# Gathers by index on GpSimd beside the second and third products of a graph network's second layer

## The chip, the cores and the metric

The kernel runs on one core of one Trainium2 chip. The metric is the device time of one execution in microseconds (us). The core has five engines that work side by side, each on its own list of instructions: TensorE (PE; PEld is its loading of weights), VectorE (DVE), ScalarE (ACT), GpSimd (POOL) and SyncE (SP). They wait for each other by semaphores. Transfers between the chip's memory (HBM) and the on-chip memory (SBUF) are done by 16 DMA engines; a transfer is issued from the queue of SP, ACT or POOL. Products are summed in PSUM.

## The reference

Four graph layers follow each other on x (4096 nodes x 128 features, f32) with one adjacency matrix adj (4096 x 4096, f32, mostly zeros); after each, x is replaced by the layer normalisation of x plus the layer's output.

```python
x = _layernorm(x + _L0_gnn_ref(x, adj, adj, L0_gnn_W, L0_gnn_a), axis=-1)
x = _layernorm(x + _L1_gnn_ref(x, adj, L1_gnn_W0, L1_gnn_b0, L1_gnn_W1, L1_gnn_b1), axis=-1)
x = _layernorm(x + _L2_gnn_ref(x, adj, ...), axis=-1)
x = _layernorm(x + _L3_gnn_ref(x, adj, ...), axis=-1)
```

The change is in the second layer, `_L1_gnn_ref`: two Chebyshev convolutions, each with an ELU behind it.

```python
def cheb_conv(x, L, W, b):
    Tx0 = x
    out = Tx0 @ W[0]
    Tx1 = L @ x
    out = out + Tx1 @ W[1]
    for k in range(2, W.shape[0]):      # W.shape[0] is 3
        Tx2 = 2.0 * (L @ Tx1) - Tx0
        out = out + Tx2 @ W[k]
        Tx0, Tx1 = (Tx1, Tx2)
    return out + b
h = jax.nn.elu(cheb_conv(x, L, W0, b0))     # 128 -> 256 features
h = jax.nn.elu(cheb_conv(h, L, W1, b1))     # 256 -> 128
```

Here L is adj. The first convolution multiplies adj by x and then by the result. The second is rearranged by the kernel: the weights are applied before adj, so it too takes two products of adj with a 4096 x 128 matrix. The layer therefore has four such products. The third layer is graph attention over 4 heads, the fourth a mean over neighbours.

## The kernel before

**Tiles.** x lies in SBUF as 128 partitions x 32 tiles of 128 features, beside its transpose xT. adj doesn't fit into SBUF, and each product reads it again, in chunks of 1 MB (`chunk`, L125 to L131): 512 rows by 512 columns, as 4 tiles of 128 rows. A chunk is loaded from SP's queue into one of five buffers of the pool `ld`; the load waits until the matmuls that read the buffer's last contents are done.

**The four products.** `propagate` (L656 to L668) runs one product: for each of 8 blocks of 512 columns it takes 8 chunks, and for each chunk 4 matmuls of 128x512, all summed in one PSUM tile, and then hands the block to the loop that called it. The first product (loop at L678) multiplies by x, and each block is transposed and copied to t1 by DVE (L681). The second (L684) multiplies by t1; in each block PE also applies the weights W1A (L690), ACT and DVE do the ELU (`elu`, L648), PE applies w2x (L695), and DVE copies the result to v (L697). The third (L707) multiplies by v; each block is transposed and copied to w by DVE (L711). The fourth is in the next part (L1126), where its blocks stand between the first steps of the third layer.

**The order of the work.** In this part a scheduler places the instructions, by the order of the program and their dependencies; instructions in `tc.keep_in_program_order` keep the order in which they are written. From the fourth product on, the order of PE, DVE, ACT and POOL is written out by hand (L1044). POOL's instructions of that part are the addition of a bias row to a block of x (L775, first of all), then products of attention weights with adj (L891, L892, L897, L898), and additions to x (L940).

**Memory that is used again.** The pools `l1w` and `l1h` hold the second layer's tiles. They are closed before the pool `l2w` of the third layer is opened, which uses the same memory: a tile of `l2w` (D, tau and others) waits for the last users of what lay there. The tiles t1, w and acc3 share one place (tag "yn"), as do v and hc (tag "v").

**What the change touches.** The lines before the loop at L678 (`wd`, `w2x`), and the ends of the three loops (after L681, L697 and L715). The first layer ends with the normalisation of x, block by block (`normalize`, L145 to L152; `normalize_x`, L154), whose last blocks are still done while the first product runs.

Of the kernel before, what the change touches and what calls it, by code (L numbers as in the profile page):

```python
# [11 lines left out]
F32 = mybir.dt.float32  # L12
BF16 = mybir.dt.bfloat16
I32 = mybir.dt.int32
AF = mybir.ActivationFunctionType
ALU = mybir.AluOpType
# [3 lines left out]
P = 128  # L20
IB = 512
TB = IB // P
# [11 lines left out]
def adj_resnorm_d4(ctx: ExitStack, tc: tile.TileContext, x_in, xT_in, adj, adjT, w0g, w0gT, a0, w1a, b1a,  # L34
# [7 lines left out]
    nc = tc.nc  # L42
    N, F = x_in.shape
# [17 lines left out]
    x = state.tile([P, NT, F], F32, name="x")  # L61
# [63 lines left out]
    def chunk(pool, src, ib, c, name="chunk", pinned=False):  # L125

        t = pool.tile([P, TB, IB], F32, name=name)
        r = nc.sync.dma_start(t, src[ib, c])
        if pinned:
            tc.keep_in_program_order(r)  # L130
        return t  # L131

    def transpose4(pool, name, src, order=lambda r: r):

        p = pool.tile([P, TB, P], F32, name=name)
        for k in range(TB):
            order(nc.tensor.transpose(p[:, k, :], src(k), ident))  # L137
        return p
# [486 lines left out]
    def network(usual):  # L625

        with ExitStack() as whole:
# [3 lines left out]
            with ExitStack() as first, ExitStack() as l1h_pool:  # L631
                ps_acc, ps_tr, ps_mm = [first.enter_context(tc.tile_pool(name=n, bufs=2, space=PSUM, reuse_waits="tile"))
                                        for n in ("ps_acc", "ps_tr", "ps_mm")]
                if not usual:
                    layer0_general(ps_acc, ps_tr, ps_mm)
                    finished = list(range(NB))
                ld = enter(name="ld", bufs=5)
                if usual:
                    finished = layer0(ld, ps_acc, ps_tr, ps_mm)
                dv = state.tile([96, N], BF16, name="dv")  # L640
                l1w = l1h_pool.enter_context(tc.tile_pool(name="l1w", bufs=2, reuse_waits="tile"))
                l1h = l1h_pool.enter_context(tc.tile_pool(name="l1h", bufs=1, reuse_waits="tile"))
                W1A = l1h.tile([P, 3, HID], F32, name="W1A")
                nc.scalar.dma_start(W1A, w1a.rearrange("k p f -> p k f"))
                W1B = l1h.tile([P, 3 * HH, F], F32, name="W1B")
                nc.scalar.dma_start(W1B, w1b.rearrange("k (h p) f -> p (k h) f", p=P))

                def elu(dst, p, bias):  # L648
                    r = l1w.tile([P, IB], F32, name="elu_r")
                    n = l1w.tile([P, IB], F32, name="elu_n")  # L650
                    nc.scalar.activation(r, p, AF.Relu, bias=bias)
                    nc.vector.tensor_scalar(n, p, bias, 0.0, op0=ALU.add, op1=ALU.min)
                    nc.scalar.activation(n, n, AF.Exp)
                    nc.vector.scalar_tensor_tensor(dst, n, -1.0, r, op0=ALU.add, op1=ALU.add)

                def propagate(stationary, order=range(NB), beside=None):  # L656


                    for ib in range(NB):
                        p = ps_acc.tile([P, IB], F32, name="pacc")  # L660
                        for n, c in enumerate(order):
                            a = chunk(ld, adjT, ib, c)
                            for k in range(TB):
                                nc.tensor.matmul(p, stationary(c * TB + k), a[:, k, :], start=n == 0 and k == 0,  # L664
                                                 stop=n == NB - 1 and k == TB - 1)
                            if beside and n == 0:
                                beside(p, ib)
                        yield ib, slice(ib * IB, (ib + 1) * IB), p  # L668

                t1 = state.tile([P, NT, F], F32, name="t1", tag="yn")  # L670
                t1T = l1h.tile([P, N], F32, name="t1T")
                hT = l1h.tile([P, HH, N], F32, name="hT")
                wd = l1h.tile([P, HH, F], F32, name="wd")
                nc.vector.tensor_sub(wd, W1B[:, 0:HH, :], W1B[:, 2 * HH:3 * HH, :])
                w2x = l1h.tile([P, HH, F], F32, name="w2x")
                nc.vector.tensor_scalar_mul(w2x, W1B[:, 2 * HH:3 * HH, :], 2.0)

                for ib, blk, p in propagate(lambda jt: x[:, jt, :], finished):  # L678
                    nc.scalar.copy(t1T[:, blk], p)
                    q = transpose4(ps_tr, "ptr", lambda k: t1T[:, (ib * TB + k) * P:(ib * TB + k + 1) * P])  # L680
                    nc.vector.tensor_copy(t1[:, ib * TB:(ib + 1) * TB, :], q)  # L681

                v = state.tile([P, NT, F], F32, name="v")
                for ib, blk, p in propagate(lambda jt: t1[:, jt, :]):  # L684
                    t2T = l1w.tile([P, IB], F32, name="t2T")
                    nc.vector.scalar_tensor_tensor(t2T, p, 2.0, xT[:, blk], op0=ALU.mult, op1=ALU.subtract)
                    for hh in range(HH):
                        ph = ps_mm.tile([P, IB], F32, name="pmm")
                        for k, r in enumerate((xT[:, blk], t1T[:, blk], t2T)):
                            nc.tensor.matmul(ph, W1A[:, k, hh * P:(hh + 1) * P], r, start=k == 0, stop=k == 2)  # L690
                        elu(hT[:, hh, blk], ph, B1A[:, hh:hh + 1])
                    q = ps_tr.tile([P, TB, F], F32, name="ptr")
                    for k in range(TB):
                        for hh in range(HH):
                            nc.tensor.matmul(q[:, k, :], hT[:, hh, (ib * TB + k) * P:(ib * TB + k + 1) * P],  # L695
                                             w2x[:, hh, :], start=hh == 0, stop=hh == HH - 1)
                    nc.vector.tensor_copy(v[:, ib * TB:(ib + 1) * TB, :], q)  # L697


                w = state.tile([P, NT, F], F32, name="w", tag="yn")  # L700
                h0T = xT

                def times_w1(p, ib):
                    for hh in range(HH):
                        nc.tensor.matmul(p, W1B[:, HH + hh, :], hT[:, hh, ib * IB:(ib + 1) * IB], start=False, stop=False)

                for ib, blk, p in propagate(lambda jt: v[:, jt, :], beside=times_w1):  # L707
                    lvT = l1w.tile([P, IB], F32, name="t2T")
                    nc.scalar.copy(lvT, p)
                    q = transpose4(ps_tr, "ptr", lambda k: lvT[:, k * P:(k + 1) * P])  # L710
                    nc.vector.tensor_copy(w[:, ib * TB:(ib + 1) * TB, :], q)  # L711
                    ph = ps_mm.tile([P, IB], F32, name="pmm")
                    for hh in range(HH):
                        nc.tensor.matmul(ph, wd[:, hh, :], hT[:, hh, blk], start=hh == 0, stop=hh == HH - 1)
                    nc.scalar.copy(h0T[:, blk], ph)  # L715

# [325 lines left out]
            with tc.manual_schedule(engines={mybir.EngineType.PE, mybir.EngineType.DVE, mybir.EngineType.Activation,  # L1044
# [68 lines left out]
                for ib in range(NB):  # L1113
                    early = ib == 1
                    p = ps_nd.tile([P, IB], F32, name="num") if early else ps_p.tile([P, IB], F32, name="pp")
# [65 lines left out]
            for _ in layer3_product(this.blocks):  # L1181
                pass

    network(True)
    with tc.If(nc.values_load(flag[0:1, 0:1], min_val=0, max_val=P) != 0):
        network(False)
# [32 lines left out]
```

## Time and profile before

| | us |
|---|---|
| median of 2 runs | 2216.26 |
| the two runs | 2214.03, 2218.48 |
| span of the profiled execution, first to last instruction | 2213.3 |
| time of the profiled execution apart from its span | not recorded; the runs lie 0.7 and 5.2 above the span |
| PE busy | 2139.9 |
| DVE busy | 1186.3 |
| POOL busy | 857.6 |
| ACT busy | 562.4 |
| first product, first to last matmul begins | 324.1 to 551.1 |
| second product | 551.5 to 819.9 |
| third product | 825.5 to 1075.9 |
| first POOL instruction after the start-up (L775) | 1115.7 |

How to read the profile. Times in it count from the span's start. A row of slices cuts the span into 40 equal parts of 55 us; each digit is the busy share in tenths. A row of the table of groups gives the line, the engine, the operation, the tiles (output <- inputs) and the count, then the busy time in us, the mean time of one in ns, and the idle time of the engine just before. In the table of waits a row says which queue or line waited for which, the total in us, how often, and the longest. The DMA table gives a row for each kind of transfer: how many, the size of each, and the median time from issue to landing. Where POOL issues a DMA, the issue isn't counted as busy.

### The profile page before, as it was taken

The numbers are of one execution on the slowest core, as the hardware profiler recorded it, in microseconds if no ns is written. First come the engines' busy times: TensorE is split into PE (matmuls) and PEld (weight loads), VectorE is DVE, ScalarE is ACT, GpSimd is POOL, SyncE is SP. The second block draws the span as 40 slices with busy tenths as digits, with TensorE's granted clock in tenths as the row PEclk, the third lists the DMA queues.
The fourth block names the chain that finished last, engine by engine and source line by source line (L and its number), as shares of the span: only waits on it lengthen the run. The fifth ranks groups of instructions, "written<-read, shape, count | busy, mean of one in ns | idle before, by whom it ended". The sixth has DMA issues, their size and how long they took to land. (4 is left out here: it accounts for less than half of the span.)

```text
span 2213.3 us, 22997 instructions
## 1 busy us (share of the span) xinstructions
PE 2139.9 (97%) x8644; PEld 850.8 (38%) x8644; DVE 1186.3 (54%) x1832; ACT 562.4 (25%) x1014; POOL 857.6 (39%) x539
## 2 busy tenths in 40 slices
PE   8999999999999999999999999979999899989997
PEld 3444454444444444444443333322222222333333
DVE  5655460000010110000026877899999999999995
ACT  6755100000000000000043223245333433332213
POOL 0000000000000000000004766698999999999980
PEclk9999999999999999999999999999999999999999
DMA  9886658888767677778876556525666566635545
GB/s 395 334 326 226 228 195 287 300 299 302 265 229 266 230 242 266 262 261 274 283 251 241 195 203 232 209 77 180 247 239 238 183 249 244 228 121 202 191 166 179
DMA packets 87145, 528.18 MB, mean 239 GB/s; under 512 B 9328, under 2 KB 15472, under 8 KB 25712
## 3 DMA queue, kind: packets, MB, share of 16 engines
q1 hardware_dynamic: 80288, 521.64, 66.8%
q10 hardware_dynamic: 6736, 4.98, 0.7%
q8 instruction: 70, 1.15, 0.2%
q14 instruction: 51, 0.42, 0.1%
HBM read 524.49 MB, written 2.10 MB: 238 GB/s over the span
## 5 line engine op out<-in xcount | busy, mean ns | idle before, releaser
L884 DVE SCALAR_TENSOR_TENSOR tau<-D,es,a 128x1024 f32<-128x1024 f32 (+1 forms) x640 | 646.4, 1058 | 44.0 <-ACT a L856 24.8
L892 POOL TENSOR_TENSOR tau<-tau,chunk 128x1024 f32<-128x1024 f32 x192 | 459.2, 2392 | 12.6 <-DVE tau L884 11.7
L775 POOL TENSOR_TENSOR x<-x,B2R 128x512 f32<-128x512 f32 x8 | 10.2, 1276 | 1145.5 <-PE px L137 1145.5
L908 PE MATMUL num<-tau,hc 128*32 128x512 f32 x2048 | 333.9, 606 | 15.0 <-POOL tau L892 9.0
L908 PE MATMUL den<-tau,cs 128*32 128x512 f32 x2048 | 343.6, 597 | 3.3 <-DVE tau L884 0.8
L999 PE MATMUL pp<-chunk,xT 128*128 128x512 f32 (+1 forms) x488 | 232.9, 607 | 0.0
L856 ACT ACTIVATE a<-chunk 128x1024 f32<-128x1024 f32 x160 | 164.2, 1026 | 254.8 <-DVE tau L890 195.1
L664 PE MATMUL pacc<-chunk,t 128*128 128x512 f32 x512 | 223.5, 592 | 0.0
L664 PE MATMUL pacc<-chunk,v 128*128 128x512 f32 x512 | 222.5, 592 | 0.0
L664 PE MATMUL pacc<-chunk,x 128*128 128x512 f32 x512 | 222.1, 592 | 0.0
L891 POOL TENSOR_TENSOR tau<-tau,chunk 128x320 f32<-128x320 f32 x192 | 167.7, 873 | 120.4 <-DVE tau L884 86.5
L1126 PE MATMUL pp<-chunk,w 128*128 128x512 f32 x448 | 204.3, 598 | 0.8 <-DVE oT L749 0.8
L379 PE MATMUL pacc<-chunk,hw 128*128 128x512 f32 x408 | 188.2, 606 | 2.4 <-DVE numT L407 1.7
L890 DVE TENSOR_TENSOR tau<-tau,a 128x704 f32<-128x704 f32 x186 | 163.1, 877 | 0.0
L898 POOL TENSOR_TENSOR tau<-tau,chunk 128x1024 f32<-128x1024 f32 x64 | 151.8, 2372 | 1.0
L908 PEld LDWEIGHTS num<-tau,hc 128*32 128x32 f32 x2048 | 62.4, 109 | 230.9 <-issue 127.8
L908 PEld LDWEIGHTS den<-tau,cs 128*32 128x32 f32 x2048 | 80.4, 110 | 177.0 <-issue 86.9
L664 PEld LDWEIGHTS pacc<-chunk,v 128*128 128x128 f32 x512 | 97.2, 190 | 122.0 <-issue 122.0
L664 PEld LDWEIGHTS pacc<-chunk,x 128*128 128x128 f32 x512 | 96.3, 190 | 115.8 <-issue 115.8
L664 PEld LDWEIGHTS pacc<-chunk,t 128*128 128x128 f32 x512 | 96.1, 190 | 115.3 <-issue 115.3
L999 PEld LDWEIGHTS pp<-chunk,xT 128*128 128x128 f32 x488 | 85.8, 190 | 133.1 <-issue 130.5
L711 DVE COPY w<-ptr 128x512 f32<-128x512 f32 x8 | 5.5, 691 | 241.5 <-PE ptr L137 241.5
(243 smaller groups left out, 1688.6 us busy)
## 6 DMA issues: line engine op xcount, KB each, us to landing
chunk<-in_adjT SPq DMA_DIRECT2D x386, 1024.0 KB, 4.9
chunk<-in_adj SPq DMA_DIRECT2D x80, 1024.0 KB, 5.0
chunk<-in_adj SPq DMA_DIRECT2D x32, 512.0 KB, 4.7
keep<-in_adjT SPq DMA_DIRECT2D x13, 1024.0 KB, 10.0
xT<-in_xT ACTq DMA_DIRECT2D x8, 256.0 KB, 6.6
out<-o ACTq DMA_DIRECT2D x7, 256.0 KB, 2.3
W1A<-in_w1a ACTq DMA_DIRECT2D x1, 384.0 KB, 5.4
W1B<-in_w1b ACTq DMA_DIRECT2D x1, 384.0 KB, 7.4
```

What stands on the lines that cost most here:

```text
L379: in_order(nc.tensor.matmul(p, hw[:, j * TB + k, :], a[:, k, :], start=first and k == 0, stop=last and k == TB - 1))
L664: nc.tensor.matmul(p, stationary(c * TB + k), a[:, k, :], start=n == 0 and k == 0, stop=n == NB - 1 and k == TB - 1)
L775: nc.gpsimd.tensor_tensor(x[:, tb, :], x[:, tb, :], B2R[:, None, :].to_broadcast([P, TB, F]), ALU.add)
L856: nc.scalar.activation(ap, a, AF.Copy, accum_out=deg[:, nt, self.mp:self.mp + 1])
L884: nc.vector.scalar_tensor_tensor(flat(tau[:, q:q + n]), flat(self.D[:, q:q + n]), es[:, nt, head:head + 1], ap, op0=ALU.max, op1=ALU.mult)
L890: nc.vector.tensor_tensor(t2[:, 0:OWN], t[:, 0:OWN], (a if only else ap)[:, 0:OWN], ALU.mult)
L891: nc.gpsimd.tensor_tensor(t2[:, OWN:WB], t[:, OWN:WB], a[:, OWN:WB], ALU.mult)
L892: nc.gpsimd.tensor_tensor(t2[:, WB:2 * WB], t[:, WB:2 * WB], a, ALU.mult)
L898: nc.gpsimd.tensor_tensor(tau2[:, 2:4, :], tau[:, 2:4, :], rep(a, 2), ALU.mult)
L908: nc.tensor.matmul(acc[32 * q:32 * q + 32, :], weights(nt, head, is_den), r[:, q, :], start=nt == 0, stop=nt == NT - 1)
L999: nc.tensor.matmul(p, y[:, c * TB + k, :], a[:, k, lo:lo + n], start=c == blocks[0] and k == 0, stop=end)
L1126: nc.tensor.matmul(p, w[:, c * TB + k, :], a[:, k, :], start=c == 0 and k == 0, stop=c == NB - 1 and k == TB - 1)
```

## The change

When the kernel runs its usual path (`usual`), it now does additional work on GpSimd, whose results nothing reads:

- ACT issues one DMA that writes x, as it stands after the first layer, to a table of 4096 rows of 128 features in HBM. POOL makes a tile of row numbers (`rows`, 31 times the partition plus the column) and fills a tile with ones.
- After each block of the three products, POOL reads one column of the block that DVE has just copied to t1, v or w (`after`); so POOL doesn't run ahead of the products.
- After blocks 2, 3, 4 and 5 of the second product, POOL issues 32 gathers: indirect DMAs that each read 64 rows of the table, chosen by a column of `rows`, into a tile of a ring of eight (`got`).
- After blocks 2, 3, 4 and 5 of the third product, POOL issues 16 gathers of 32 rows, and after each multiplies a 128x96 piece of the filled tile (`pause`).
- Beside the first product, and after the other blocks, there are no gathers.

```diff
                 nc.vector.tensor_scalar_mul(w2x, W1B[:, 2 * HH:3 * HH, :], 2.0)
 
+                if usual:
+                    rows = l1h.tile([P, 32], I32, name="rows")
+                    nc.gpsimd.iota(rows, pattern=[[1, 32]], base=0, channel_multiplier=31)
+                    table = whole.enter_context(tc.tile_pool(name="table", bufs=1, space=bass.MemoryType.DRAM)).tile([N, F], F32, name="table")
+                    nc.scalar.dma_start(table.rearrange("(t p) f -> p t f", p=P), x)
+                    fill = l1h.tile([P, 2, IB], F32, name="fill")
+                    nc.gpsimd.memset(fill, 1.0)
+                count = [0]
+
+                def beside(n, ib):
+                    if ib in (0, 1, 6, 7) or n == 0:
+                        return
+                    for k in range(16):
+                        if n == 1:
+                            gather(64)
+                            gather(64)
+                        else:
+                            gather(32)
+                            pause(96)
+
+
+                def gather(n=P, width=F):
+                    k = count[0] % 8
+                    count[0] += 1
+                    got = l1w.tile([P, F], F32, name="got", bufs=8)
+                    tc.keep_in_program_order(nc.gpsimd.indirect_dma_start(got[0:n, 0:width], None, table if width == F else table[:, 0:width], bass.IndirectOffsetOnAxis(ap=rows[0:n, k:k + 1], axis=0)))
+
+                def pause(n=IB):
+                    tc.keep_in_program_order(nc.gpsimd.tensor_tensor(fill[:, 0, 0:n], fill[:, 0, 0:n], fill[:, 1, 0:n], ALU.mult))
+
+                def after(tile, ib):
+                    tc.keep_in_program_order(nc.gpsimd.tensor_copy(fill[:, 0, 0:1], tile[:, ib * TB, 0:1]))
+
                 for ib, blk, p in propagate(lambda jt: x[:, jt, :], finished):
...
                     nc.vector.tensor_copy(t1[:, ib * TB:(ib + 1) * TB, :], q)
+                    if usual:
+                        after(t1, ib)
+                        beside(0, ib)
...
                     nc.vector.tensor_copy(v[:, ib * TB:(ib + 1) * TB, :], q)
+                    if usual:
+                        after(v, ib)
+                        beside(1, ib)
...
                     nc.scalar.copy(h0T[:, blk], ph)
+                    if usual:
+                        after(w, ib)
+                        beside(2, ib)
```

## The prediction

> **What bounds the kernel now.** I read the page first: its span, the busy table and the row of slices.
>
> ```profile
> span 2213.3 us, 22997 instructions
> PE 2139.9 (97%) x8644; PEld 850.8 (38%) x8644; DVE 1186.3 (54%) x1832; ACT 562.4 (25%) x1014; POOL 857.6 (39%) x539
> ...
> PE   8999999999999999999999999979999899989997
> ...
> POOL 0000000000000000000004766698999999999980
> ...
> L664 PE MATMUL pacc<-chunk,t 128*128 128x512 f32 x512 | 223.5, 592 | 0.0
> ```
>
> PE is busy for 97% of the span. POOL (GpSimd) has nothing to do for the first half, and from slice 21 on it is a loaded engine. The second layer's three products (L664) have no idle time ahead of their matmuls.
>
> Then the busy time by stretch. The columns are the stretch, its length, busy time of PE, PEld, DVE, ACT and POOL, granted clock, share of the DMA engines, GB/s. I cut where the gathers will begin and end.
>
> ```profile
> 552.00:660.00 108.00, 108.00 (x292) 50.94 (x291) 13.44 (x19) 9.45 (x14) 0.00 (x0) 1.00 0.73 249
> 660.00:797.00 137.00, 137.00 (x368) 64.65 (x367) 16.91 (x24) 10.53 (x16) 0.00 (x0) 1.00 0.72 244
> ...
> 921.00:1047.00 126.00, 126.00 (x306) 56.15 (x305) 3.04 (x5) 4.68 (x8) 0.00 (x0) 1.00 0.78 267
> ```
>
> PE is busy for the whole of each stretch at full clock, POOL for none of it, and the DMA engines have 28% and 22% to spare. Next, who the loads of chunks wait for (the SP queue's waits), and how long one takes (the DMA table).
>
> ```profile
> SPq L128 <- PE pacc L664: 670.4, 191, 8.4
> ...
> chunk<-in_adjT SPq DMA_DIRECT2D x386, 1024.0 KB, 4.9
> ```
>
> The loads wait for PE to release a buffer, not the reverse: 670 us in total. One chunk lands in 4.9 us. The v copies (L697) of the second product are 34.4 us apart, so a chunk lasts 4.3 us; with five buffers a load is issued four chunks, 17.2 us, ahead of its use. 17.2 - 4.9 = 12.3 us of slack. These stretches are bound by PE alone.
>
> [...] The trace of before has no DMA from POOL[...]. [...] W1A and W1B from the ACT queue landed in 5.4 and 7.4 us beside the chunk stream. [...]
>
> **The change part by part.** The built program keeps the order of PE, DVE and SP exactly; ACT gains one instruction, POOL gains all the others.
>
> 1. The table. ACT issues one DMA of x (2 MB, 4096 rows of 512 B) after the last normalisation, L151 at 334.3 to 335.4 us. It waits for DVE; behind it on ACT stands the last xT copy (L158, at 336.40). The issue of the x load of the same shape took 0.84 us on SP (L534), so that copy moves by under 1 us; xT is first read at 579.5 (L690). Zero on the path. The write shares the DMA engines with the chunk stream. The x load, the same bytes, landed in 13.0 us; I allow 13 to 25 for the table, so it ends by 361. In the built program one chunk load reuses the table's semaphore and waits for it: the one issued at 363.48 in the trace of before. That is 28 us after the table's issue, and 12 us of prefetch stand behind it (less in this product, where a chunk lasts 3.4 us: 4 x 3.4 - 4.9 = 8.8). The table would have to take 37 us to stop PE. The first gather waits for it too, 300 us later. Cost 0; the upper bound, a table of 45 us, would cost 8.
>
> 2. Set-up and touches on POOL: an iota, a memset, and 24 one-column copies that wait for a block of t1, v or w. The least POOL operations in the trace take 0.1 us; all sit in idle POOL time. Because t1 and w share a buffer, the first w copy on DVE (858.0) waits for POOL's read of the last t1 block, done soon after 553.8, before any gather. The first hc product (L797, 1119.8) waits for POOL's touch of the last v block, which stands behind the 128 gathers of 64 rows. The first copy of D (L872, ACT, 1129.6) waits for the last gathers, because its memory is theirs; queued behind it on ACT is the ELU of the next block (L751), for whose result PE waits. These are the deadlines.
>
> 3. 128 gathers of 64 rows, 32 after each of blocks 2 to 5 of the second product: gates at 659.6, 694.0, 728.4, 762.8 (ends of the v copies). POOL's time for one isn't in the trace. From below: 0.33 us, what SP takes to issue a chunk. [...] So 32 us per block of 34.4; the last end at 762.8 + 32 = 795. [...]
>
> 4. 64 gathers of 32 rows, each followed by a 128x96 multiply, 16 after each of blocks 2 to 5 of the third product (w copies end at 921.5, 952.9, 984.3, 1015.8). The multiply, from POOL's own rows of 320 and 448 elements (873 and 1144 ns): 2.12 ns an element, so 873 - 224 x 2.12 = 398 ns. One pair 1.4 us, 22 us in a block of 31.4; the end at 1038. [...] POOL is next wanted at 1115.7 (L775). So even unoverlapped the POOL work ends in time: zero on the path.
>
> 5. The bytes. 64 rows of 512 B; 512 B packets of the W1B load took 28 ns each, so 64 x 28 / 16 = 0.11 us of the 16 engines per gather (an estimate), 3.6 us per block where 34.4 x 0.28 = 9.6 us are free. In the third product 16 x 0.056 = 0.9 of 6.9. Share of DMA 0.72 to 0.83 and 0.78 to 0.81; the first product runs at 0.87 with PE at 227.2 of 228 us. PE is not starved. From below a gain is excluded: nothing is taken away and no engine's order changes.
>
> 6. [...] In each block of the second product PE waits for two results of L654, which reads two SBUF tiles; the trace leaves 0.7 and 1.4 us between them and the matmuls of L695. If a gather held L654 for its full 1.0 us, PE would lose up to 0.3 us for the first and, carried on, about 1 us per block: 0 to 4 us in four blocks. I take 1.
>
> Sum: 2213.3 + 1 on the span. The runs' median, 2216.26, stands 3.0 above the span and the lowest run, 2214.03, 0.7; the profiled execution's own time isn't given apart, so I put the change on the median: **2217 us**. 2% either way, some 44 us, is about what a measurement of this kernel can tell from no change; the two runs differ by 0.2%.
>
> **Rivals.**
> - *No change, as above*, 2211 to 2224, 0.86. It includes the case that the gathers don't fill the blocks they are named for: at 0.33 us they end after a third of each block, above 1.07 us they run on into blocks that were to be free. Neither moves the time.
> - *Slower: the chunk stream starves.* Place: blocks 3 to 6 of the second product. If a gather keeps the 16 engines from the chunks for longer than its bytes need, the free time is gone at 9.6/32 = 0.30 us per gather; from there PE waits for chunks. [...] At 1.0 us: 4 x 22.4 - 12 = 78 and 4 x 9.1 - 12 = 24: 2318. For it: the packets are small and many[...]. Against it: small packets in the trace took 28 ns beside the stream. Its likeliest time 2270 (0.75 us); chance 0.10, of which 0.06 past 2%.
> - *Slower: POOL is late.* Its work must end by 1129.6: 128 g + 64 (g + 0.4) = 470, so g = 2.31 us decides. At g = 3: 659.6 + 384 + 218 = 1261, 132 us late, some 10 of it covered by ACT's wait for L751: 2338. For it: the prices on POOL are rough. [...] Chance 0.03.
> - Faster by over 2%: 0.01, with no mechanism.
>
> **How the numbers follow.** The range is 2211 to 2238: the first case and the mild end of the second, where gathers cost between 0.30 and about 0.5 us of the engines. That holds 0.83. Slower by over 2%: 0.06 + 0.03 = 0.09; faster 0.01; within 0.90.
>
> **What the profile after would show.** POOL busy or issuing in slices 12 to 18; the v copies still 34.4 us apart in blocks 3 to 6, the w copies 31.4; no idle ahead of L664; DMA share 0.8 in 660 to 797; chunk loads landing in about 5 to 6 us; the first D copy at 1129 to 1132 and not ended by a DMA. I am wrong if PE waits for chunk loads in 660 to 797, if POOL's last gather ends after 1120, or if the chunk load at 363.48 waits for the table.

## The result: slower, and PE waits in the second product

The changed kernel takes 2309.86 us (median of two runs, 2309.81 and 2309.92) where the kernel before took 2216.26: a ratio of 1.0431, 95% interval 1.0414 to 1.0448. The forecast was 2217, with a range of 2211 to 2238. The prediction was wrong, and on the slow side by 93 us.

The page of the changed kernel, its head and three of its groups:

```profile
span 2307.8 us, 23327 instructions
...
PE 2152.3 (93%) x8644; PEld 854.8 (37%) x8644; DVE 1186.4 (51%) x1832; ACT 562.5 (24%) x1014; POOL 1062.9 (46%) x821
...
PE   8999999999986667999999999987999899989998
...
POOL 0000000000045451026400566779999999999990
PEclk9999999999997888999999999999999999999999
...
L664 PE MATMUL pacc<-chunk,t 128*128 128x512 f32 x512 | 223.5, 592 | 0.0
...
L703 POOL DMA_INDIRECT got<-table,rows x192 | 173.2, 902 | 54.2 <-issue 54.2
...
L722 DVE SCALAR_TENSOR_TENSOR t2T<-pacc,xT 128x512 f32<-128x512 f32 x8 | 5.5, 691 | 275.6 <-remote 180.6
```

PE falls to between 60 and 80% in slices 13 to 16, where the gathers stand. L664 has no idle time ahead of it, so no chunk is late. The step whose wait has grown is L722 on DVE (L686 before): it makes t2T from the sum of a block and waits for PE alone. Its releaser is given as "remote": the view names no instruction for the event that ended the wait. Gathers do count as busy on POOL, unlike what "How to read the profile" above says of DMA issues: POOL's busy time grew by 1062.9 - 857.6 = 205.3 us, and 173.2 of them are gathers.

The same by stretch, with the columns of the prediction's table:

```profile
552.00:660.00 108.00, 108.00 (x292) 50.91 (x291) 13.44 (x19) 9.71 (x14) 0.56 (x3) 1.00 0.73 249
660.00:797.00 137.00, 95.54 (x235) 43.53 (x234) 8.54 (x12) 5.27 (x8) 74.11 (x85) 0.84 0.54 186
...
1047.00:1130.00 83.00, 83.00 (x200) 36.91 (x199) 1.94 (x3) 2.93 (x5) 58.86 (x93) 1.00 0.80 272
```

Until 660 nothing has changed. Then PE is busy for 95.54 of 137 us, and the DMA engines' share falls from 0.72 to 0.54: they aren't the bound either. In the third product, with its own gathers, PE is busy all the time. The chain is in the table of waits, and in the time order of block 3:

```profile
DVE t2T L722 <- remote: 180.6, 4, 45.6
...
PE pmm L726 <- DVE t2T L722: 83.4, 4, 21.4
```

```profile
683.03 1.02 PE L726 MATMUL pmm<-xT,W1A 128*128 128x512 f32 x2
...
683.88 1.02 PE L726 MATMUL pmm<-t1T,W1A 128*128 128x512 f32 x2
...
698.58 0.90 POOL L703 DMA_INDIRECT got<-table,rows  x1 [0.30 <-issue]
704.26 0.69 DVE L722 SCALAR_TENSOR_TENSOR t2T<-pacc,xT 128x512 f32<-128x512 f32 x1 [44.38 <-remote]
...
705.01 2.08 PE L726 MATMUL pmm<-t2T,W1A 128*128 128x512 f32 x2 [20.10 <-DVE t2T L722]
```

The same step in the kernel before:

```profile
682.89 0.69 DVE L686 SCALAR_TENSOR_TENSOR t2T<-pacc,xT 128x512 f32<-128x512 f32 x1 [23.34 <-PE pacc L664]
```

PE had begun the last matmul of the block's sum before 683.03, when it began the next two matmuls in its list. In the kernel before, t2T follows the first of these two by 0.20 us, so it was due at 683.23. DVE began it at 704.26, 21 us late, and 4.8 us after the last of the 32 gathers had ended on POOL (698.58 + 0.90 = 699.48). PE had nothing else to do. Its granted clock was 1.00 from 660 to 684 and 0.50 from 690 to 710 (0.84 in the stretch, 1.00 before), and the pair of L726 took 2.08 us instead of 1.02. The v copies (L733 here) are 57.40, 58.34, 58.16 and 57.77 us apart in blocks 3 to 6 instead of 34.40, which makes 23.0 + 23.9 + 23.8 + 23.4 = 94.1 us. The span grew by 2307.8 - 2213.3 = 94.5. So everything lies in these four blocks; 83.4 us of it are PE's waits for t2T, and PE's busy time grew by 12.4.

SP's loads of chunks, which also wait for PE, are late too: issued at 676.35, 687.45 and 704.25 where before they went at 676.02, 679.45 and 682.88. The middle one, before and after:

```profile
679.45 0.33 SPq L128 DMA_DIRECT2D chunk<-in_adjT  x1
```

```profile
687.45 0.33 SPq L128 DMA_DIRECT2D chunk<-in_adjT  x1
```

These loads also show when the delay begins. Counted from the v copy, they are due at 3.43, 6.86 and so on, every 3.43 us. In all four blocks the loads up to 13.73 were on time; the one due at 17.16, with 13 gathers issued, was on time or 0.4 us late; the one due at 20.60, with 16 issued, was 7.7 to 15.2 us late. So the first 13 or so gathers of a block delay nothing that the trace shows.

What PE waits for from DVE, and DVE from ACT, is on time (PE's matmul begins 0.06 us after the end of t2T, and L652 on DVE 0.03 us after the end of L651 on ACT), though in this run that is after the gathers of the block are over (e8 below shows it beside gathers). So the question is: why does news from PE come late while POOL gathers?

### The profile page after: what moved, and what is told of

Read it like the earlier page. It is cut to its first block, busy times and chain, and to the rows that moved or that the text cites. A ratio compares the mean times of both kernels' runs of the same rounds, so it can differ in the third digit from the quotient of the medians.

```text
span 2307.8 us, 23327 instructions
## 1 busy us (share of the span) xinstructions
PE 2152.3 (93%) x8644; PEld 854.8 (37%) x8644; DVE 1186.4 (51%) x1832; ACT 562.5 (24%) x1014; POOL 1062.9 (46%) x821
## 5 line engine op out<-in xcount | busy, mean ns | idle before, releaser
L664 PE MATMUL pacc<-chunk,t 128*128 128x512 f32 x512 | 223.5, 592 | 0.0
L664 PE MATMUL pacc<-chunk,v 128*128 128x512 f32 x512 | 222.5, 592 | 0.0
L664 PE MATMUL pacc<-chunk,x 128*128 128x512 f32 x512 | 222.1, 592 | 0.0
L703 POOL DMA_INDIRECT got<-table,rows x192 | 173.2, 902 | 54.2 <-issue 54.2
L722 DVE SCALAR_TENSOR_TENSOR t2T<-pacc,xT 128x512 f32<-128x512 f32 x8 | 5.5, 691 | 275.6 <-remote 180.6
L664 PEld LDWEIGHTS pacc<-chunk,v 128*128 128x128 f32 x512 | 97.2, 190 | 122.0 <-issue 122.0
L664 PEld LDWEIGHTS pacc<-chunk,x 128*128 128x128 f32 x512 | 96.3, 190 | 115.8 <-issue 115.8
L664 PEld LDWEIGHTS pacc<-chunk,t 128*128 128x128 f32 x512 | 96.1, 190 | 115.3 <-issue 115.3
```

The lines of the kernel that those rows point to most:

```text
L703: tc.keep_in_program_order(nc.gpsimd.indirect_dma_start(got[0:n, 0:width], None, table if width == F else table[:, 0:width], bass.Indirect ...
```

## The experiments

The runs came in six groups; those of one group ran one after the other on one chip, and beside each group the kernel before took 2213.0 to 2214.8 us (2216.26 beside the result). That turned out to matter more than most of the edits, so the groups are given first. The last column says how many semaphore updates each trace has on record for the third product's 64 gathers (16 each, 1024 due).

| group | chip number | kernels and times, us | updates recorded of 1024 |
|---|---|---|---|
| result | not recorded | changed 2309.86 | 706 |
| 1 | 7 | e1 2215.18, e2 2215.54, e3 2215.68, e4 2215.23 | 1011 to 1019 |
| 2 | 8 | e5 2309.57, e6 2243.30, e7 2216.47, e8 2287.29 | 670 to 721 |
| 3 | 13 | e9 2214.40, e10 2216.95, e11 2218.04, e12 2215.24 | 1009 to 1024 |
| 4 | 11 | f1 2215.49, f2 2214.65, f3 2214.88, f4 2214.53 | 1014 to 1019 |
| 5 | 11 | g1 2309.58, g2 2309.96 | 689 to 720 |

### Group 1: which part, and is it the number or the kind of POOL's work?

e1: no gathers beside the second product.

```diff
-                    if ib in (0, 1, 6, 7) or n == 0:
+                    if ib in (0, 1, 6, 7) or n != 2:
```

> The table and the gathers of the third product alone; no gathers beside the second. Theory A (a burst of gathers keeps DVE from starting an instruction until it is over; only the second product has a DVE instruction due inside a burst): the time of before, 2214 to 2220 us, and v copies 34.4 us apart throughout. Theory B (gathers slow whatever they lie beside, through the DMA engines or the table): half-way, 2225 to 2260 us, with w copies more than 31.4 us apart.

e2: 16 gathers in a block, not 32.

```diff
                             gather(64)
-                            gather(64)
```

> 16 gathers of 64 rows per block of the second product in place of 32; the third product as after. The burst ends about 20.5 us after the v copy, at some 680 us, and t2T is due at about 683. Theory A with the hold ending with POOL's last gather: no delay, 2214 to 2220 us. Theory A with the hold lasting the 4.8 to 6.4 us beyond the last gather that the profile shows: t2T is 2 to 4 us late in each of four blocks, 2224 to 2236 us. Theory B (a cost per gather): half of the 94 us, about 2262 us.

e3: multiplies on POOL in place of gathers.

```diff
-                            gather(64)
-                            gather(64)
+                            pause(340)
+                            pause(340)
```

> In the second product each gather is replaced by a POOL multiply of 128x340 from and to SBUF, about 0.91 us, so POOL is busy for about 34 us at the same place; no gathers there; the third product as after. Theory A (it is the gathers): t2T waits for one multiply at most, 2214 to 2222 us. Theory C (any POOL work that follows without a gap keeps DVE out[...]): t2T waits for the end of the burst as after, 2290 to 2315 us.

e4: a multiply after each gather.

```diff
-                    for k in range(16):
...
+                    for k in range(26 if n == 1 else 16):
+                        gather(64 if n == 1 else 32)
+                        pause(96)
```

> In the second product 26 pairs of a gather of 64 rows and a 128x96 multiply per block in place of 32 gathers: 26 x 1.48 = 38.5 us, the length of the burst after. If an ordinary POOL instruction between two gathers lets DVE in, t2T is late by one pair at most, 2214 to 2224 us. If the hold outlasts it (it runs some 5 us past the last gather), t2T waits for the end of the burst, 2295 to 2320 us.

All four had t2T on time. I read this then as: the third product and the table are free, and only more than 16 gathers back to back do harm. The second half doesn't follow. The changed kernel itself wasn't in this group, and f1 below shows a group in which its 32 gathers do no harm either. What stands is what multiplies on POOL cost an instruction on DVE at the same time (e3, block 3):

```profile
687.38 1.17 DVE L654 SCALAR_TENSOR_TENSOR hT<-elu_n,elu_r 128x512 f32<-128x512 f32 x1 [0.69 <-ACT elu_n L653]
```

L654, with two SBUF inputs, takes 1.17 us beside POOL's multiplies instead of 0.69; it made 0.4 us per block (v copies 34.8 us apart instead of 34.4).

### Group 2: is DVE held, or PE's news?

e5: the changed kernel, with one matmul and one DVE instruction more, some 9.5 us after the gathers begin, each block with other operands (PSUM to PSUM, PSUM to SBUF, SBUF to PSUM, two SBUF inputs).

```diff
+                            if probe and n == 3:
+                                probe(ib)
...
+                    q = ps_tr.tile([P, IB], F32, name="ptr")
+                    nc.tensor.matmul(q, ident, xT[:, 0:IB], start=True, stop=True)
+                    if ib == 3:
+                        nc.vector.tensor_scalar(q, q, 2.0, None, op0=ALU.mult)
...
+                    else:
+                        nc.vector.tensor_tensor(q, mine[:, 0, :], mine[:, 1, :], ALU.mult)
```

> The kernel after, with one more matmul and one DVE instruction of 128x512 in the middle of each of the four bursts of the second product, some 13 us into it: in blocks 3, 4, 5, 6 from PSUM to PSUM; from PSUM to SBUF; from SBUF to PSUM; from two SBUF tiles to PSUM. Theory A1 [...]: the first isn't delayed, and at least the last is, to the end of the burst; t2T as after, total 2300 to 2320 us. Theory A2 (the hold keeps DVE from starting anything): all four wait to the end of their bursts. If an instruction with at most one SBUF side were free, t2T (PSUM and one SBUF tile in) couldn't be held, so I expect the second or the third to be held too.

2309.57 us, as the changed kernel. The first and the last of the added DVE instructions, by tile (shortest, median and longest time in ns; first and last start in us):

```profile
L732 DVE TENSOR_SCALAR ptr<-ptr x1: 699/699/699, 669.2 to 669.2; 128x512 f32<-128x512 f32 x1
...
L738 DVE TENSOR_TENSOR ptr<-mine x1: 772/772/772, 843.6 to 843.6; 128x512 f32<-128x512 f32 x1
```

All four ran during the gathers, 0.04 us after the end of the matmul that they waited for, and took 0.69 to 0.77 us; t2T of the same blocks was late. So at that point, 9.5 us in and with 8 gathers issued, DVE wasn't held and PE's news still arrived. The delay sets in later, after some 13 to 16 gathers, so these four can't say whether DVE is held from then on. What speaks against it in the changed kernel is that SP's loads, which wait for PE and not for DVE, are late too.

e6: 20 gathers per block, and from block 4 on one multiply behind them.

```diff
+                    if n == 1:
+                        for k in range(20):
+                            gather(64)
+                        if ib > 3:
+                            pause(96)
+                        return
```

> 20 gathers of 64 rows per block in the second product, whose last ends about 1.6 us after t2T is due; after blocks 2 and 3 nothing follows them, after blocks 4 and 5 one 128x96 multiply. If the end of the gathers frees DVE: t2T about 2 us late in all four, 2222 to 2228 us. If DVE, once held, stays held some 5 us beyond the last gather as after: 6 to 8 us late in the first two; and if an ordinary POOL instruction frees it, about 2 us in the last two: 2230 to 2240 us.

2243.30 us. Two blocks, without and with the multiply:

```profile
684.17 0.90 POOL L705 DMA_INDIRECT got<-table,rows  x1 [0.31 <-issue]
...
689.19 0.69 DVE L724 SCALAR_TENSOR_TENSOR t2T<-pacc,xT 128x512 f32<-128x512 f32 x1 [29.13 <-remote]
```

```profile
766.96 0.40 POOL L708 TENSOR_TENSOR fill<-fill 128x96 f32<-128x96 f32 x1
...
771.21 0.69 DVE L724 SCALAR_TENSOR_TENSOR t2T<-pacc,xT 128x512 f32<-128x512 f32 x1 [28.93 <-remote]
```

t2T begins 4.1 to 4.3 us after the end of POOL's last gather in all four blocks, whether POOL then multiplies or not. It follows the end of the burst of gathers. The v copies are 41.0 to 41.2 us apart, so with 12 gathers fewer the loss is 6.6 to 6.8 us per block instead of 23.0 to 23.9.

e7: plain DMAs of 64 neighbouring rows from POOL, in place of gathers.

```diff
+                def plain(n):
+                    k = count[0] % 8
...
+                    tc.keep_in_program_order(nc.gpsimd.dma_start(got[0:n, :], table[k * n:(k + 1) * n, :]))
```

> The 32 gathers per block of the second product replaced by 32 plain DMAs of 64 rows of the table issued from POOL. Theory A [...]: as after, 2290 to 2320 us if the burst reaches t2T, 24 us after its start. Theory A by the reading of the indices (only an indirect DMA does it): the time of before, 2214 to 2220 us.

2216.47 us, t2T at 681.95. This was in a group where gathers did harm, so it counts: the same number of transfers of the same bytes from the same queue, not indirect, leaves PE's news alone. In blocks 4 to 6 t2T alone couldn't tell, because POOL had begun the last of its 32 DMAs by 21.3 us after the v copy and t2T is due at 24.04. But SP's load due at 20.60 was on time in all four blocks, where in the changed kernel it was 7.7 us late or more. The plain DMAs weren't spaced as the gathers are (0.52 us each on POOL, and then waits for their landings), so the kind of DMA and the pace aren't told apart by it.

e8: a multiply of one column after each gather.

```diff
                             gather(64)
+                            pause(1)
                             gather(64)
+                            pause(1)
```

> All gathers of the kernel after, 32 of 64 rows per block, each followed by a multiply of one column. If any ordinary POOL instruction between gathers lets DVE in: the time of before, ratio 0.998 to 1.003, though the bursts are now longer (some 43 us). If it was the length of the 128x96 multiply, 0.4 us, that let DVE in: as after, ratio 1.03 to 1.06.

2287.29 us (2284.11 to 2289.12), ratio 1.0332 (1.0314 to 1.0349). Spaced by 1.30 instead of 1.21 us the gathers still do harm, but in block 3 mainly in another place: t2T began 1.25 us after PE's next matmul (681.48, 682.73; in f1 below 0.20 us), so some 1 us late, and then the ELU's first step on ACT, which waits for PE too, was late twice.

```profile
691.95 0.69 ACT L651 ACTIVATE elu_r<-pmm,B1A 128x512 f32<-128x512 f32 x1 [37.33 <-remote]
...
692.67 0.75 DVE L652 TENSOR_SCALAR elu_n<-pmm,B1A 128x512 f32<-128x512 f32 x1 [9.25 <-ACT elu_r L651]
...
694.12 0.69 DVE L654 SCALAR_TENSOR_TENSOR hT<-elu_n,elu_r 128x512 f32<-128x512 f32 x1 [0.70 <-issue]
...
700.19 0.93 POOL L705 DMA_INDIRECT got<-table,rows  x1 [0.15 <-issue]
...
703.15 0.69 ACT L651 ACTIVATE elu_r<-pmm,B1A 128x512 f32<-128x512 f32 x1 [9.07 <-remote]
```

Between the two late steps, with gathers going on until 701.12, DVE began L652 0.03 us after ACT's step had ended, and L654, which has two SBUF inputs, took its 0.69 us. So DVE isn't held here, and ACT's news reaches it. DVE's news reaches PE too: PE's next matmul (L733) began at 694.96, 0.15 us after the end of L654. What is late is news from PE: ACT's two late steps began 7.3 and 16.0 us after the end of the matmuls that they wait for, where in the kernel before it is 0.10 us. The victim is any wait for PE that falls due late in a burst, on DVE, ACT or SP.

### Group 3: a backlog of landings?

My theory then was a backlog: gathers are issued every 1.21 us, but land more slowly, and PE's news waits for them. The 1.4 us from landing to landing in the expectations below is not what the changed kernel's trace shows. There, in block 3, the packets of the 32 gathers begin 1.21 us apart on average (662.68 to 700.19), each gather's 0.71 to 3.35 us after its end on POOL, and over 0.73 us only where chunks are moving as well.

e9: two buffers for gathered rows; e10 and e12: 16 and 128 rows in a gather.

```diff
-                    got = l1w.tile([P, F], F32, name="got", bufs=8)
+                    got = l1w.tile([P, F], F32, name="got", bufs=2)
```

> The changed kernel with two buffers for the gathered rows instead of eight, so that each gather waits for the landing of the gather two before it; all 32 gathers of 64 rows per block stay. Theory D (gathers land every 1.4 us and are issued every 1.21 us; while gathers that were issued have not landed, PE's signals are held back): no more than two gathers are ever outstanding, so nothing is held, t2T on time at about 683, v copies 34.4 apart, 2215 to 2225. Rival C (it is the number of gathers in a row, whatever their spacing): t2T is held until the burst is over, here at 660.9 + 32 x 1.4 = 706 or later, 2310 or more. Rival R (it is the rate at which they land, which stays at one per 1.4 us): as C.

```diff
-                            gather(64)
-                            gather(64)
+                            gather(16)
+                            gather(16)
```

> The changed kernel with 32 gathers of 16 rows per block in place of 32 of 64 rows, eight buffers as before. If a gather's landing costs 1.4 us whatever its rows (theory D with a price per gather): t2T at 704 as in the changed kernel, about 2310. If the 1.4 us are for the rows or their bytes (a quarter of them here, 0.35 us): gathers land as fast as they are issued, t2T at 683, 2215.

```diff
-                            gather(64)
-                            gather(64)
+                            gather(128)
+                            gather(128)
```

> The changed kernel with 32 gathers of 128 rows per block in place of 32 of 64 rows. Price per gather (theory D): as the changed kernel, t2T at 704, about 2310. Price per row: a gather lands every 2.8 us, the 32 of a block last 90 us, POOL waits for its eight buffers, and t2T of block 3 is held until 750 or later; the time is 2400 or more.

e11: no loads of chunks in blocks 3 to 6 of the second product.

```diff
-                            a = chunk(ld, adjT, ib, c)
+                            if ib not in again:
+                                a = chunk(ld, adjT, ib, c)
```

> The changed kernel with the chunk loads of blocks 3 to 6 of the second product left out: these blocks multiply by the chunk that is loaded last before them, so the chunk stream is silent beside the gathers (the result is another one). If gathers land slowly because they share the DMA engines with the chunk stream (theory D with contention): they land within their 1.21 us, no backlog, t2T at 683, v copies 34.4 apart, 2215. If gathers are slow or hold PE's signals by themselves: t2T at about 704, v copies 57 apart, about 2310.

None of the four lost anything: 2214.40, 2216.95, 2215.24 and 2218.04 us. Each alone would have looked like a cure. Four different cures at once, 128 rows among them (0.97 us a gather on POOL instead of 0.90), were the sign that the edits weren't what differed. A backlog of transfers is ruled out by the changed kernel's own trace: the packets of block 3's 32 gathers moved between 662.7 and 700.6, so the last had moved 1.2 us after POOL was done with it (699.48), and t2T still waited until 704.26. Whether signals pile up somewhere else isn't shown.

### Groups 4 and 5: the program, the chip, or the occasion

f1: 40 one-column multiplies on POOL at set-up, where POOL is idle; they only shift where its later instructions lie. f2 and f3: 32 and 96 rows. f4: four buffers.

```diff
                     nc.gpsimd.memset(fill, 1.0)
+                    for k in range(40):
+                        pause(1)
```

> The changed kernel with 40 multiplies of one column put on POOL at set-up, long before the gathers, where POOL is idle: they shift where POOL's instructions lie and nothing else. Theory S (32 back-to-back gathers of 64 rows do it as such): as the changed kernel, about 2310, t2T of block 3 at 704. Rival L (an accident of where this one program's instructions lie): the hold is gone, about 2216.

```diff
-                            gather(64)
-                            gather(64)
+                            gather(32)
+                            gather(32)
```

> The changed kernel with 32 gathers of 32 rows per block in place of 32 of 64. If 64 rows are a special size (128 and 16 rows showed no hold): about 2216. If the hold grows with the rate at which gathers are issued and 64 rows aren't special (32 rows are issued every 1.19 us, between 1.15 and 1.21): about 2310. If it needs both a rate and a number of rows, part of it: 2230 to 2290.

```diff
-                            gather(64)
-                            gather(64)
+                            gather(96)
+                            gather(96)
```

> The changed kernel with 32 gathers of 96 rows per block in place of 32 of 64. If 64 rows are a special size: about 2216. If the hold is lost only with 128 rows (all partitions written): about 2310.

```diff
-                    got = l1w.tile([P, F], F32, name="got", bufs=8)
+                    got = l1w.tile([P, F], F32, name="got", bufs=4)
```

> The changed kernel with four buffers for the gathered rows instead of eight: a gather waits for the landing of the gather four before it; the gathers wait for gaps in the chunk stream for up to 3.4 us, so up to three or four are outstanding at once. If the number outstanding decides (eight allowed: held, two: not held): between 2216 and 2310, and nearer 2216. If only the spacing on POOL decides, it stays near 1.21 us: about 2310.

All four again as the kernel before. For f1 that leaves the place of the instructions, or the occasion. So the last two runs were the changed kernel without an edit (g1), and f1's program once more (g2), side by side.

> The changed kernel itself, not a line different, on another chip than before. Theory K (the hold comes with the chip or the session, not with the kernel alone): the time is one of two, 2310 as in the result or about 2216, and on this chip the shifted program gives the same one. Theory L (it is fixed by where this program's instructions lie): 2310 on every chip. The time 2216 here would rule out L and every cause that lies in the program alone; 2310 leaves both, and the shifted program, sent with it to the same chip, decides.

> The changed kernel with 40 multiplies of one column on POOL at set-up, as before, now on the same chip as the changed kernel itself. Theory K: the same time as that, within 3 us, whichever it is. Theory L: about 2216 where the changed kernel has 2310.

g1: 2309.58 us (2309.07 to 2310.26), ratio 1.0428 (1.0410 to 1.0445). g2: 2309.96 (2308.44 to 2310.59), ratio 1.0431 (1.0413 to 1.0448). The place of the instructions is out. And f1 and g2 are the same program: 2215.49 us in one group and 2309.96 in another, under the same chip number, 11. Their traces are the cleanest comparison of the case. f1, time order and stretch:

```profile
682.54 0.69 DVE L724 SCALAR_TENSOR_TENSOR t2T<-pacc,xT 128x512 f32<-128x512 f32 x1 [23.34 <-PE pacc L664]
```

```profile
660.00:797.00 137.00, 137.00 (x368) 64.81 (x367) 17.08 (x24) 10.53 (x16) 103.40 (x115) 1.00 0.79 270
```

g2:

```profile
703.45 0.69 DVE L724 SCALAR_TENSOR_TENSOR t2T<-pacc,xT 128x512 f32<-128x512 f32 x1 [44.59 <-remote]
```

```profile
660.00:797.00 137.00, 95.17 (x238) 43.65 (x237) 8.54 (x12) 5.27 (x8) 75.37 (x86) 0.85 0.54 181
```

Before the gathers the two agree. Beside them, f1 is what the prediction described, with PE busy for all of the 137 us, and g2 is the result over again. POOL's own times agree; the landings can't be compared. The group row and the DMA rows (the last number is the time from issue to landing) of f1:

```profile
L708 POOL DMA_INDIRECT got<-table,rows x192 | 174.2, 907 | 53.4 <-issue 53.4
...
got<-table,rows POOLq DMA_INDIRECT x192, 4.9
```

and of g2:

```profile
L708 POOL DMA_INDIRECT got<-table,rows x192 | 172.8, 900 | 54.4 <-issue 54.4
...
got<-table,rows POOLq DMA_INDIRECT x192
```

g2 has no landing time, because most records of the gathers' semaphore updates are missing: 296 of 2048 in the second product, against 2022 in f1. This is the mark that the table's last column shows. In the groups where PE's news was late, gathers lose records even in the third product, where they cost nothing: 670 to 721 of 1024, against 1009 to 1024 in the other groups. e7 bears the mark there too (670), while its plain DMAs in the second product kept 2048 of 2048 records. So the mark goes with the occasion and with indirect DMAs, not with late news as such.

What sets a group's condition isn't in the record. In each marked group some kernel was run several times, in each unmarked one none was; three of each kind are too few to lean on, and e5, e6 and e7, run once each in a marked group, bear the mark too.

In the changed kernel's trace PE's matmuls begin on time at 683.03, and the update that DVE waits for is recorded at 704.2. The time is lost between these two, where no record lies. Missing records and late updates come in the same groups; whether the one has to do with the other isn't shown. Every run of this case carries a span and a granted clock, so none shows what the kernel does when nothing is recorded.

**What is shown, and what is open.** Shown: the changed kernel loses its 94 us because waits for PE end late while gathers follow each other on POOL every 1.21 us, and only on some occasions (the result and groups 2 and 5); on another the same program lost nothing. In the same groups as these losses the kernel before, and e7 with plain DMAs, lost nothing. Open: by which path gathers delay PE's signal, whether the recording has a part in it, and what brings the condition about. The edits of groups 1, 3 and 4 can't say which rows, spacing or buffers would help in the marked condition; apart from f1's, run again as g2, none was tried there.

No kernel tried was faster than the kernel before.

## Why the prediction was wrong, step by step

1. *The table, cost 0.* Right. In f1 it landed in 20.9 us (I had allowed 13 to 25), and the chunk load at 363.48 didn't wait for it (363.13 in f1, where all of this stage stands 0.35 us earlier).
2. *Touches and deadlines.* Right. The added work on POOL held up nothing behind the second product: even with the delay, the third product's stretch shown above has PE busy 83.00 of 83.00 us, and in f1 the first D copy is at 1129.55 (1129.61 before). In the changed kernel POOL's last gather ended at 1134.3, after the 1120 that I had named as a sign of being wrong, but only because the third product began 94 us later; in f1 it ended at 1039.5.
3. *Gathers of 64 rows: 1.0 us each, "zero on the path".* This is the step that failed. The 1.0 us was an assumption of mine, as the trace of before has no DMA from POOL. It was near: 0.90 us and a gap of 0.30, so 32 x 1.21 = 39 us, longer than the block of 34.4, and in f1 the last ended at 816, long before its deadline. But "zero on the path" rested on POOL's deadlines alone. The term that I had put at 0 measures 94.1 us, 23.0 to 23.9 in each of four blocks, and it is no work of POOL's that PE waits for: PE's own signal is late at DVE, and PE then waits for DVE's t2T. I had listed what the gathers wait for and who waits for them, and taken every other wait as untouched.
4. *Pairs of 32 rows and a multiply.* Right: 0.409 us for the multiply (predicted 0.398), 1.47 us for a pair (1.4), w copies 31.3 to 31.7 us apart in g2 and f1, nothing lost in either condition. That is weaker than it looks: there are only 16 gathers in a block, the number around which the delay sets in beside the second product, and the last of them ended 2.9 to 5.5 us before ACT's wait for PE was over (the changed kernel). SP's loads beside them were on time too.
5. *Bytes, PE not starved.* Right. With the gathers the DMA share is 0.79 (f1); up to 0.83 was predicted. A gather of 64 rows moved as 16 packets of 2048 B, 84 ns each at the median, and 16 of 4 B, 9 ns each: 0.09 us of each engine. The price of 0.11 came from 64 packets of 512 B, so it was near with another make-up. The sentence that a gain is excluded because "no engine's order changes" is true, but I let it stand for the other side as well: the same order doesn't mean the same times.
6. *L654 held by gathers, 0 to 4 us, taken as 1.* No trace of before showed such a hold; it was an assumption. In f1, L654 took 0.69 us in each of these blocks, beside gathers: 0. In the runs here it was longer beside multiplies (1.17 us in e3).

*The rivals.* "The chunk stream starves" named the place, blocks 3 to 6 of the second product, and would have been read from the same slices; but L664 never waited and the DMA engines had more time free than before. "POOL is late" fell with 0.90 us a gather, 1.21 with its gap, against the 2.31 that it needed. None named the mechanism. With 0.90 on a time within 2%, I had left it no room: of the gathers the trace of before showed nothing, and I bounded only their duration, not what such a transfer does to others. The chances don't agree among themselves either: the range of 2211 to 2238 was given 0.83, less than the 0.86 of the first case that lies inside it.

## What to carry to other kernels

Indirect DMAs issued over and over from POOL cost a stage that shares no data with them (94.1 us in four blocks here): read who is late before asking who is busy, and look for waits whose releaser the trace can't name. In the condition in which gathers of 64 rows 1.21 and 1.30 us apart cost 3 to 4%, plain DMAs (e7) and bursts of 16 gathers of 32 rows 1.47 us apart (the third product) cost nothing. Whether the latter is due to the rows, the spacing or the shortness of the burst isn't shown; a longer burst of them wasn't tried in that condition. And when an edit makes a loss vanish, run the unedited kernel beside it in the same group before believing the edit: here three groups of edits looked like cures or bounds, and weren't shown to be any.

## What the runs showed that I had not expected

- One program, two times, 2215.49 (one run) and 2309.96 us (four runs within 0.1%), with the kernel before at 2213.5 and 2214.2 beside them.
- While gathers run in the marked condition, PE's signals come late: at DVE by up to 22.7 us (block 3 of g1), at SP by 7.7 to 15.2 us (the loads due at 20.60 in the changed kernel), at ACT 7.3 and 16.0 us after the end of the matmuls (e8). DVE's and ACT's signals don't: 0.15 us from DVE to PE and 0.03 us from ACT to DVE (e8). The delay isn't there from the start: it sets in after some 13 to 16 gathers at 1.21 us, in g1, g2 and e6 as in the changed kernel.
- A gather's time on POOL hardly depends on its rows. The groups of the second product's stretch for 16 and 128 rows (e10, e12):

```profile
L703 POOL DMA_INDIRECT got<-table,rows x117 | 100.2, 856 | 35.6 <-issue 35.3 <-DVE v L733 0.3
```

```profile
L703 POOL DMA_INDIRECT got<-table,rows x109 | 105.1, 965 | 33.1 <-issue 33.1
```

  0.86 us for 16 rows, 0.97 for 128, eight times as many.
